# A decoder of four gated blocks: one-hot places by four comparisons, and the shared expert's fill in front of the slot list

## The chip, the cores and the metric

The kernel runs on one core of a Trainium2 chip. A core has TensorE (PE, matrix products into PSUM; PEld is its weight load), VectorE (DVE), ScalarE (ACT), GpSimd (POOL) and SyncE (SP), which work side by side and wait for one another by semaphores. DMA queues move data; GpSimd also issues the gathers. The metric is the device time of one launch in microseconds, lower is better. The kernel before takes 1079.16 us, the median of three runs (1078.13 to 1082.75).

## The reference

Sixteen blocks of 128 tokens with 256 features (`x`) pass through four pairs of a cross-attention-like layer and a feed-forward layer, each added to `x` with a learned gate:

```python
x = x + jnp.tanh(g_xattn[0]) * _L0_xattn_ref(ctx_2048, ctx_2048, _layernorm(x, axis=-1), ...)
x = x + jnp.tanh(g_ffn[0]) * _L0_ffn_ref(_layernorm(x, axis=-1), ...)
...
x = x + jnp.tanh(g_ffn[2]) * _L2_ffn_ref(_layernorm(x, axis=-1), ...)
```

Two of the feed-forward layers, number 0 and number 2, are mixtures of experts: for each of the 2048 tokens the two best of eight experts are taken, each expert is a gated product of width 176, and a shared expert that every token passes through is added. Number 2 in short:

```python
scores = jnp.sqrt(jax.nn.softplus(xt.astype(jnp.float32) @ gate_w.T))
_, idx = jax.lax.top_k(scores + gate_b, K)
weights = jnp.take_along_axis(scores, idx, axis=1) * ROUTE_SCALE
...
y = y + _expert(xt, w1[e], w2[e], w3[e], cw[:, e])   # for every expert e
z = _expert(xt, sw1, sw2, sw3)                       # the shared expert
return (y + z).reshape(Bx, Sx, D)
```

## The kernel before

The kernel goes through the eight layers as stages. The change lies in the two routed stages, `stage_moe0` (line 458, "stage one" in the prediction) and `stage_moe2` (line 739, "stage two"), and in the helper `spots` (line 387) that both call.

A routed stage does not multiply every token by every expert. It sorts token-expert pairs into 40 blocks of 128 slots, each block of one expert, gathers the tokens of a block from DRAM and multiplies them by that expert's weights. Its steps are:

- For four groups of four token blocks: `stats` and `normal` (VectorE; the power of -0.5 on GpSimd) write the normalised group `xn`, which SP also writes to DRAM (`xs`); `turn` transposes it on TensorE (tile `tx`) and copies it to `xT`; `logit` multiplies it by the gate weights into `lg`. In stage two `turn` also splits each value into a rounded part (ScalarE, line 736) and a rest (VectorE, line 737), and a group's scores are 16 products of 16 columns.
- `route`: from the scores the two best experts of each token (`first_two`), then `spots`. In stage two the route begins with three small functions on ScalarE (Exp at line 812, Ln, Exp), which are in VectorE's way.
- `spots`: the two best as a mask `mb`; TensorE counts by a triangular matrix (`pc`, line 395); from the counts come each pair's slot `ps`, its block `blk` and its place in the block `place`. Then the list of slots is made by a product: `inb` (line 421) says for each token and pair which of the 40 blocks it is in (128x1280, one or zero), `inp` (line 431) says for each token which of the 128 places it has, times the token's number. TensorE adds the 32 products into `w` (line 436): place by block, with the token's number in it. `who` (line 437) is that as an integer list, which steers the gathers (`load`, lines 593 and 848). `offs` (line 445) is the list of experts.
- The 20 double blocks: `load`, `block_turn` (tile `tb`), `block_up`, the hidden transposition (`tg`), `block_down` (`yb`).

The shared expert needs no list, so its work is cut into portions that are put where TensorE has to wait; the helper `fill` issues the next portion. In stage two there are ten portions for eight pairs of token blocks. Portion p multiplies pair p up (`up`, tile `ub`, eight products of 352 columns), transposes the hidden values of pair p-1 (`hidden`, tile `tg`) and multiplies pair p-2 down (`down`, tile `yb`). Unless a portion is called late, its hidden values go through ScalarE (`sil`, `gcopy`, two copies of `tg`, `ysh`) and GpSimd (`hid`, line 890; `hT`, line 905; the addition to `x`, line 941); a late one uses VectorE in GpSimd's place.

The order on TensorE, VectorE and ScalarE is the order of the calls in the source (`tc.manual_schedule`); each engine works off its instructions in that order. `route` and `spots` are generators: every `yield` is a place at which the caller may put a fill. In stage one a portion stands in each turn of the group loop, and the others around the route. In stage two before the change all ten portions stand behind the last scores: two behind the route's top, two behind the counts, two among the four rounds of `inp`, and the last four, late, behind the list.

PSUM tiles come from two pools: four buffers for `tx`, `lg`, `pc`, `w`, `tg` and `yb`, two for `ub`. `inp` has three buffers, shared with `xn`.

Of the kernel before, what the change touches and what calls it, by code (L numbers as in the profile page):

```python
# [10 lines left out]
F32 = mybir.dt.float32  # L11
# [3 lines left out]
ALU = mybir.AluOpType  # L15
# [3 lines left out]
P = 128  # L19
B = 16  # L20
# [35 lines left out]
def passage(ctx: ExitStack, tc: tile.TileContext, a: dict, out: bass.AP, inv, flag):  # L56
# [109 lines left out]
    def bc(ap, axis, n):  # L166

        u = ap.unsqueeze(axis)
        shape = list(u.shape)
        shape[axis] = n  # L170
        return u.to_broadcast(shape)
# [215 lines left out]
    def spots(mr, mo, psa, cn, one, pos, who, offs, inb):  # L387

        f, g = "p t e -> p (t e)", "p e t -> p (e t)"
        mb = mr.tile([P, B, E], BF16, name="mb")  # L390
        nc.vector.tensor_tensor(mb, one[:, 0], one[:, 1], ALU.add)
        yield
        pc = psa.tile([P, 2, B, E], F32, name="pc", tag="a")
        for i, w in enumerate((cn["upper"], cn["onesb"])):
            nc.tensor.matmul(pc[:, i].rearrange(f), lhsT=w, rhs=mb.rearrange(f), start=True, stop=True)
        cnt = mr.tile([P, E, B], F32, name="cnt")
        nc.vector.tensor_copy(cnt, pc[:, 1].rearrange("p t e -> p e t"))
        run = mr.tile([P, E, B], F32, name="run")
        nc.vector.tensor_tensor_scan(run.rearrange(g), cn["ct"].rearrange(g), cnt.rearrange(g), 0.0, ALU.mult, ALU.add)
        nb = mr.tile([P, E], F32, name="nb")  # L400
        nc.vector.tensor_scalar(nb, run[:, :, B - 1], 1.0 / P, 0.49609375, ALU.mult, ALU.add)
        nc.vector.tensor_scalar(nb, nb, MAGIC, None, ALU.add)
        nc.vector.tensor_scalar(nb, nb, MAGIC, None, ALU.subtract)
        be = mr.tile([P, E], F32, name="be")
        nc.vector.tensor_tensor_scan(be, ones[:, 0:E], nb, 0.0, ALU.mult, ALU.add)
        nc.vector.tensor_tensor(nb, be, nb, ALU.subtract)
        nc.vector.tensor_tensor(run, run, cnt, ALU.subtract)
        nc.vector.scalar_tensor_tensor(run, bc(nb, 2, B), float(P), run, ALU.mult, ALU.add)
        at = mr.tile([P, B, E], F32, name="at")
        nc.vector.tensor_tensor(at, pc[:, 0], run.rearrange("p e t -> p t e"), ALU.add)  # L410
        ps = mr.tile([P, 2, B], F32, name="ps")
        nc.vector.tensor_tensor(one, one, bc(at, 1, 2), ALU.mult)
        nc.vector.tensor_reduce(ps, one, AX.X, ALU.add)

        blk = mr.tile([P, 2, B], F32, name="blk")
        nc.vector.tensor_scalar(blk, ps, 1.0 / P, -0.49609375, ALU.mult, ALU.add)
        nc.vector.tensor_scalar(blk, blk, MAGIC, None, ALU.add)
        nc.vector.tensor_scalar(blk, blk, MAGIC, None, ALU.subtract)
        at = mr.tile([P, 2, B], F32, name="place")
        nc.vector.scalar_tensor_tensor(at, blk, -float(P), ps, ALU.mult, ALU.add)  # L420
        nc.vector.tensor_tensor(
            inb, bc(blk.rearrange("p i t -> p (i t)"), 2, NBLK), bc(cn["block"], 1, 2 * B), ALU.is_equal
        )
        yield

        w = psa.tile([P, NBLK], F32, name="w", tag="a")
        for q in range(0, 2 * B, 8):
            inp = mo.tile([P, 8, P], F32R, name="inp", tag="xn", bufs=3)
            for n in range(8):
                i, t = divmod(q + n, B)  # L430
                nc.vector.tensor_scalar(
                    inp[:, n], cn["slot"], at[:, i, t : t + 1], cn["token"][:, t : t + 1], ALU.is_equal, ALU.mult
                )
            yield
            for n in range(8):
                nc.tensor.matmul(w, lhsT=inp[:, n], rhs=inb[:, q + n], start=(q + n == 0), stop=(q + n == 2 * B - 1))
        nc.vector.tensor_scalar(who, w, B * P - 1.0, None, ALU.min)
        nc.vector.tensor_copy(pos, ps)

        le = mr.tile([1, NBLK, E], F32, name="le")  # L440
        jf = mr.tile([1, NBLK], F32, name="jf")
        nc.vector.tensor_tensor(le, bc(be[0:1], 1, NBLK), bc(cn["block"][0:1], 2, E), ALU.is_le)
        nc.vector.tensor_reduce(jf, le, AX.X, ALU.add)
        nc.vector.tensor_scalar(jf, jf, E - 1.0, float(WE), ALU.min, ALU.mult)
        nc.vector.tensor_copy(offs, jf)
# [293 lines left out]
    def stage_moe2(kv1, we, gw, gb, tgc, pos, wgt, cn, xs, ys):  # L739
# [4 lines left out]
        with tc.tile_pool(name="mr", bufs=1) as mr, tc.tile_pool(name="mo", bufs=2) as mo, tc.tile_pool(  # L744
# [34 lines left out]
            def turn(g):  # L779
                xn = xns.pop(g)  # L780
                for c in range(2):
                    t = psa.tile([P, GB * P], F32, name="tx", tag="a")
                    for k in range(GB):
                        nc.tensor.transpose(t[:, k * P : (k + 1) * P], xn[:, k, c * P : (c + 1) * P], ident)
                    split(xTs[g][:, c, 0], xTs[g][:, c, 1], t)
# [4 lines left out]
            def logit(g):  # L790
                for b in range(g * GB, (g + 1) * GB):
                    for n in range(4):
                        nc.tensor.matmul(
                            lg[:, b].rearrange("p a e -> p (a e)"),
                            lhsT=token(b, n // 2, n % 2),
                            rhs=gws[:, n // 2].rearrange("p a e -> p (a e)"),
                            start=(n == 0),
                            stop=(n == 3),
                        )
# [5 lines left out]
            def route():  # L805

                t3 = lambda n: mr.tile([P, B, E], F32, name=n)
                l, u, w, z, sc, sq, bi = [t3(n) for n in ("l", "u", "w", "z", "sc", "sq", "bi")]
                nc.vector.tensor_copy(l, lg[:, :, 1, :])
                nc.vector.tensor_tensor(l, l, lg[:, :, 0, :], ALU.add)  # L810
                nc.vector.scalar_tensor_tensor(u, l, -1.0, l, ALU.mult, ALU.max)
                nc.scalar.activation(u, u, AF.Exp, scale=-1.0)

                nc.vector.tensor_scalar(w, u, 1.0, None, ALU.add)
                nc.scalar.activation(sq, w, AF.Ln)
                nc.vector.tensor_scalar(w, w, -1.0, None, ALU.add)
                nc.vector.tensor_scalar(z, w, 0.0, None, ALU.is_equal)
                nc.vector.tensor_tensor(w, w, z, ALU.add)
                nc.vector.reciprocal(w, w)
                nc.vector.tensor_scalar(sc, l, 0.0, None, ALU.max)  # L820
                nc.vector.tensor_tensor(sq, sq, w, ALU.mult)
                nc.vector.tensor_tensor(sq, sq, z, ALU.add)
                nc.vector.tensor_tensor(u, u, sq, ALU.mult)
                nc.vector.tensor_tensor(sc, sc, u, ALU.add)

                nc.scalar.activation(sq, sc, AF.Ln)
                nc.scalar.activation(sq, sq, AF.Exp, scale=0.5)
                nc.vector.tensor_scalar(sq, sq, 1e-30, None, ALU.max)
                nc.vector.reciprocal(w, sq)
                nc.vector.tensor_tensor(w, w, sc, ALU.mult)  # L830
                nc.vector.tensor_tensor(sq, sq, w, ALU.add)
                nc.vector.tensor_scalar(sq, sq, 0.5, None, ALU.mult)
                nc.vector.tensor_tensor(bi, sq, bc(gb, 1, B), ALU.add)
                mx = mr.tile([P, 2, B], F32, name="mx")
                one = first_two(mr, cn, bi, mx, -BIG)
                yield
                gate = mr.tile([P, 2, B, E], F32, name="gate")
                nc.vector.tensor_tensor(gate, one, bc(sq, 1, 2), ALU.mult)
                nc.vector.tensor_reduce(wgt, gate, AX.X, ALU.add)
                nc.vector.tensor_scalar(wgt, wgt, tg[:, tgc : tgc + 1], None, ALU.mult)  # L840
                yield from spots(mr, mo, psa, cn, one, pos, who, offs, inb)
# [111 lines left out]
            for g in range(1, NG):  # L953
                if g + 1 < NG:
                    stats(g + 1)
                normal(g)
                logit(g - 1)
                turn(g)
            logit(NG - 1)
            r = route()  # L960
            next(r)
            fill()
            fill()
            next(r)
            next(r)
            fill()
            fill()
            for n in range(4):
                next(r)
                if n % 2 == 0:  # L970
                    fill()
            next(r, None)
            n = NBLK // 2
            for s in range(4):
                load(s)
# [1089 lines left out]
```

## Time and profile before

| What | us |
|---|---|
| median of three runs | 1079.16 |
| the profiled execution, its time | 1077.04 |
| its span, first to last instruction | 1075.3 |
| TensorE busy | 904.1 (84%) |
| VectorE busy | 607.5 (56%) |
| ScalarE busy | 456.8 (42%) |
| GpSimd busy | 342.3 (32%) |
| stage two: first `stats` | 584.2 |
| stage two: last scores end | 614.8 |
| stage two: `who` | 656.9 |
| stage two: first `tb` | 671.8 |
| stage one: last scores end | 166.0 |
| stage one: `who` | 195.5 |
| stage one: first `tb` | 207.5 |

A line of the timeline gives the start, the busy time, the engine, the source line, the operation, the tiles it writes and reads, the shape, and in brackets the idle time before it with what ended it. Busy times of pipelined matrix products overlap, so the distance from start to start is the better price of a piece. "PEclk" is the clock that TensorE was granted, as a share of the full one. The parts beside the stages in the table, the attention of the other layers, are not touched by the change.

### The profile page before, as it was taken

To read this page: it belongs to the slowest core of one execution; us is meant where nothing else is said; L and a number is where in the kernel's file an instruction comes from. 1 tells how busy PE (TensorE), PEld (TensorE's weight loads), DVE (VectorE), ACT (ScalarE), POOL (GpSimd) and SP (SyncE) were. 2 spreads that over 40 slices of the span, in tenths; PEclk is the share of its full clock that TensorE was granted. 3 is DMA by queue.
4 is the path that set the end of the run, shared out by engine and by line. 5 is a ranking of instruction groups with operands and counts; after the bars stand their busy time and mean duration, and the time that the engine had idled before them with its cause. 6 is when DMAs were issued, how large, how long until landed. Compare 5 with 4: busy or idle time off the path is not lost. (4 is left out here: it accounts for less than half of the span.)

```text
span 1075.3 us, 14892 instructions
## 1 busy us (share of the span) xinstructions
PE 904.1 (84%) x5212; PEld 602.5 (56%) x5212; DVE 607.5 (56%) x1537; ACT 456.8 (42%) x707; POOL 342.3 (32%) x389
## 2 busy tenths in 40 slices
PE   3899978899999888888864858998169999998797
PEld 1444456677778444455443747887145555555564
DVE  5988966322225656787788586454345555534442
ACT  1211024223322446666762242454257777882111
POOL 5766322543115324211111046550443342201000
PEclk9999979999999978999986557899579999997999
DMA  9100070233341109800000202352488887530000
GB/s 305 41 1 1 0 220 21 63 104 109 69 143 50 39 20 144 78 1 1 1 1 1 78 1 88 109 145 82 142 247 235 220 222 195 164 79 1 20 30 32
DMA packets 71401, 94.12 MB, mean 88 GB/s; under 512 B 9271, under 2 KB 63127, under 8 KB 69015
## 3 DMA queue, kind: packets, MB, share of 16 engines
q1 hardware_dynamic: 56952, 67.21, 21.1%
q0 software_dynamic: 14080, 23.78, 11.4%
q10 hardware_dynamic: 288, 2.10, 0.5%
q8 instruction: 45, 0.74, 0.3%
q14 instruction: 36, 0.29, 0.1%
HBM read 57.06 MB, written 33.55 MB: 84 GB/s over the span
## 5 line engine op out<-in xcount | busy, mean ns | idle before, releaser
L1667 ACT ACTIVATE pt<-s 128x1024 f32<-128x1024 f32 x128 | 126.4, 1024 | 32.5 <-PE s L1660 29.8
L709 POOL DMA_INDIRECT yc<-ys,pos x64 | 62.4, 975 | 125.0 <-DVE x L729 49.2
L297 PE MATMUL y<-kv,toep 128*128 128x512 f32 x192 | 86.6, 602 | 1.6 <-DVE toep L237 1.6
L1660 PE MATMUL s<-qa,ka 64*128 64x256 f32 x512 | 64.3, 332 | 8.3 <-ACT pt L1667 7.5
L1676 PE MATMUL av<-pt,v 128*32 128x256 f32 x1024 | 69.4, 389 | 0.1
L289 POOL TENSOR_TENSOR kv<-ctxT 128x1024 f32<-128x1024 f32 x32 | 60.2, 1900 | 28.3 <-PE y L297 28.3
L1660 PEld LDWEIGHTS s<-qa,ka 64*128 64x128 f32 x512 | 38.6, 188 | 46.9 <-issue 23.2
L1687 DVE COPY avs<-av 128x256 f32<-128x256 f32 x64 | 27.1, 423 | 65.5 <-PE av L1676 48.5
L297 PEld LDWEIGHTS y<-kv,toep 128*128 128x128 f32 x192 | 35.6, 192 | 43.7 <-issue 40.3
L616 PE MATMUL ub<-L0we,xbT 128*128 x160 | 50.8, 460 | 2.6 <-ACT xbT L607 2.6
L593 POOL DMA_INDIRECT xb<-xs,who x40 | 38.2, 954 | 43.3 <-PE tb L605 33.2
L913 PE MATMUL yb<-L2we,hT 88*128 (+1 forms) x224 | 41.7, 315 | 9.6 <-DVE hT L737 3.9
L848 POOL DMA_INDIRECT xb<-xs,who x40 | 38.1, 953 | 31.7 <-PE tb L860 20.9
L302 DVE TENSOR_TENSOR pr<-y,qT 128x1024 f32<-128x1024 f32 x32 | 39.0, 1222 | 12.1 <-PE y L297 9.4
L1567 POOL TENSOR_TENSOR hl<-f,hl 128x512 fp32r<-128x512 f32 x16 | 20.5, 1282 | 79.5 <-ACT hl L1566 79.5
L477 PE MATMUL up<-L0s,xT 128*128 128x352 f32 x128 | 43.0, 482 | 0.0
L913 PEld LDWEIGHTS yb<-L2we,hT 88*128 88x128 f32 x224 | 33.6, 205 | 16.5 <-DVE hT L737 9.0
L1086 PE MATMUL s<-qa,ka 18*128 18x512 f32 x128 | 37.4, 660 | 4.9 <-ACT follow L1380 4.9
L305 DVE TENSOR_REDUCE oT<-pr 128x128 f32<-128x1024 f32 x32 | 38.9, 1219 | 1.0
L1676 PEld LDWEIGHTS av<-pt,v 128*32 128x32 f32 x1024 | 26.9, 110 | 20.4 <-issue 0.7
L642 PE MATMUL yb<-L0we,hTb 88*128 x160 | 37.9, 379 | 0.0
L616 PEld LDWEIGHTS ub<-L0we,xbT 128*128 128x128 f32 x160 | 28.8, 190 | 15.5 <-ACT xbT L607 2.8
(384 smaller groups left out, 2043.1 us busy)
## 6 DMA issues: line engine op xcount, KB each, us to landing
scr<-hl SPq DMA_DIRECT2D x64, 256.0 KB
ys<-ysb SPq DMA_DIRECT2D x40, 256.0 KB
qa<-scr SPq DMA_DIRECT2D x32, 256.0 KB
ka<-scr SPq DMA_DIRECT2D x32, 256.0 KB
L2we<-in_L_w_dram POOLq DMA_DIRECT2D x6, 792.0 KB
L0we<-in_L_w_dram SPq DMA_DIRECT2D x6, 704.0 KB
xs<-xn SPq DMA_DIRECT2D x8, 512.0 KB
x<-in_x_dram SPq DMA_DIRECT2D x4, 512.0 KB
```

The costliest lines, as they stand in the source:

```text
L289: nc.gpsimd.tensor_tensor(t, bc(ch, 3, 8), bc(ch, 2, 8), ALU.mult)
L297: nc.tensor.matmul(y[:, ns], lhsT=T[:, h, d : d + P], rhs=kv[mc][:, ns], start=(mc == 0), stop=(mc == lc))
L302: nc.vector.tensor_tensor(pr, y.rearrange("p (b j i) -> p b j i", b=B, j=8), bc(qT[:, lc, :, hs], 2, 8), ALU.mult)
L305: nc.vector.tensor_reduce(oT[:, lc, :, hs], pr, AX.X, ALU.add)
L477: nc.tensor.matmul(t[:, n, 0 : 2 * I], lhsT=xT[:, c, b * P : (b + 1) * P], rhs=s13[:, c, n, :], start=(c == 0), stop=(c == 1),)
L593: nc.gpsimd.indirect_dma_start(out=xbs[s][:, i, :], out_offset=None, in_=xs, in_offset=bass.IndirectOffsetOnAxis(ap=who[:, 2 * s + i : 2 * ...
L616: nc.tensor.matmul(t[:, i, 0 : 2 * I], lhsT=xbT[:, i, c, :], rhs=we[:, bass.ds(regs[s][i] + c * 2 * I, 2 * I)], start=(c == 0), stop=(c == 1),
L709: nc.gpsimd.indirect_dma_start(out=got[b][:, i, :], out_offset=None, in_=ys, in_offset=bass.IndirectOffsetOnAxis(ap=pos[:, i, b : b + 1], ...
L913: nc.tensor.matmul(y[:, i, :], lhsT=hT[:, x, k, i, :], rhs=we[0:HI, bass.ds(at[i] + 4 * I + k * D, D)], start=(n == 0), stop=(n == 3),)
L1660: nc.tensor.matmul(s[:, h, jj, :], lhsT=ka[r, 2 * i + jj, sc * P : (sc + 1) * P], rhs=qa[r, 2 * i + jj, :], start=True, stop=True,)
L1667: nc.scalar.activation(pts[b, i][:, sc], s, AF.Exp)
L1676: nc.tensor.matmul(av[c : c + 32, :], lhsT=va[:, sc, 8 * h + 2 * i + jj, :], rhs=pt[:, sc, h, jj, :], start=(sc == 0), stop=(sc == 1),)
```

## The change

Two things are changed.

In `spots`, which both stages call, the token's number moves from `inp` to `inb`: two products of 128x640 in place multiply `inb` by it, and `inp` becomes a plain one-hot tile, made eight places at a time by one comparison of 128x1024 whose two operands are broadcast. Thirty-two instructions with two scalars each become four with two tensors each. TensorE's 32 products into `w` stay.

In `stage_moe2` the portions of the shared expert move. Two are now issued in each of the three turns of the group loop, one on either side of `turn`; one stands behind the last scores and in front of the route's top; the last three stand behind the route's top. From there the counts, `inb`, the four rounds of `inp` and the list follow with nothing between them. No portion is late any more, so all ten use ScalarE and GpSimd.

```diff
         nc.vector.tensor_tensor(
             inb, bc(blk.rearrange("p i t -> p (i t)"), 2, NBLK), bc(cn["block"], 1, 2 * B), ALU.is_equal
         )
+        for i in range(2):
+            u = inb[:, i * B : (i + 1) * B]
+            nc.vector.tensor_tensor(u, u.bitcast(F32), bc(cn["token"], 2, NBLK), ALU.mult)
         yield
 
         w = psa.tile([P, NBLK], F32, name="w", tag="a")
         for q in range(0, 2 * B, 8):
             inp = mo.tile([P, 8, P], F32R, name="inp", tag="xn", bufs=3)
-            for n in range(8):
-                i, t = divmod(q + n, B)
-                nc.vector.tensor_scalar(
-                    inp[:, n], cn["slot"], at[:, i, t : t + 1], cn["token"][:, t : t + 1], ALU.is_equal, ALU.mult
-                )
+            i, t = divmod(q, B)
+            nc.vector.tensor_tensor(inp, bc(at[:, i, t : t + 8], 2, P), bc(cn["slot"], 1, 8), ALU.is_equal)
             yield
...
                 normal(g)
                 logit(g - 1)
+                fill()
                 turn(g)
+                fill()
             logit(NG - 1)
             r = route()
+            fill()
             next(r)
             fill()
             fill()
-            next(r)
-            next(r)
             fill()
-            fill()
-            for n in range(4):
-                next(r)
-                if n % 2 == 0:
-                    fill()
-            next(r, None)
+            for _ in r:
+                pass
```

## The prediction

> **What bounds the kernel now.** I read the page first: the span, and the slices of TensorE's busy time and granted clock. "Slot list" below is the tile `who`; "stage one" is the first routed stage, "stage two" the second.
>
> ```profile
> span 1075.3 us, 14892 instructions
> PE   3899978899999888888864858998169999998797
> PEclk9999979999999978999986557899579999997999
> ```
>
> A slice is 26.9 us. TensorE is nearly full almost everywhere; the thin part is slices 22 to 26, which hold stage two, and there the clock is low as well. Then stretches of time (columns: length, busy us and instructions of PE, PEld, DVE, ACT, POOL, then PE clock, DMA share, GB/s), the last line from stage one:
>
> ```profile
> 595.70:602.00 6.30, 5.69 (x26) 5.00 (x25) 4.78 (x16) 1.17 (x2) 1.13 (x2) 0.50 0.26 86
> 620.00:626.00 6.00, 0.00 (x0) 0.00 (x0) 3.70 (x11) 3.99 (x6) 0.96 (x1) 0.50 0.00 0
> 150.00:155.00 5.00, 5.00 (x34) 4.10 (x33) 0.92 (x3) 1.97 (x5) 2.09 (x2) 1.00 0.99 248
> ```
>
> While stage two turns and scores the tokens, TensorE is busy 90% of the time yet has the half clock: so a slot that looks free there is not. During the top of the route it stands idle. The timeline of stage two gives the order of what ends last:
>
> ```profile
> 611.85 2.94 PE L793 MATMUL lg<-gws,xT 128*128 128x16 f32 x13 [0.26 <-DVE xT L737]
> 615.81 0.31 ACT L812 ACTIVATE u<-u 128x128 f32<-128x128 f32 x1 [3.44 <-DVE u L811]
> 631.74 0.29 PE L395 MATMUL pc<-mb,upper 128*128 128x128 bf16 x1 [2.13 <-DVE mb L391]
> 638.07 2.26 POOL L890 TENSOR_TENSOR hid<-gcopy,sil 128x352 f32<-128x352 f32 x1 [0.62 <-ACT gcopy L889]
> 639.47 17.07 DVE L431 TENSOR_SCALAR inp<-slot,place,token 128x128 fp32r<-128x128 f32 x32
> 656.91 0.20 DVE L437 TENSOR_SCALAR who<-w 128x40 uint32<-128x40 f32 x1 [0.38 <-PE w L436]
> 671.78 1.91 PE L860 MATMUL tb<-ident,xb 128*128 128x128 f32 x8
> ```
>
> From 614.8 to 656.9 VectorE carries the path. From 656.9 to 671.8 TensorE works off four fills and stands 3.30 us. From 689.8 the blocks run every 3.66 us at full clock. Stage one's timeline differs:
>
> ```profile
> 177.93 8.66 DVE L431 TENSOR_SCALAR inp<-slot,place,token 128x128 fp32r<-128x128 f32 x24
> 187.54 2.12 PE L436 MATMUL w<-inb,inp 128*128 128x40 f32 x16
> 188.81 2.75 DVE L431 TENSOR_SCALAR inp<-slot,place,token 128x128 fp32r<-128x128 f32 x8 [2.22 <-PE w L436]
> 195.48 0.20 DVE L437 TENSOR_SCALAR who<-w 128x40 uint32<-128x40 f32 x1 [3.92 <-PE w L436]
> ```
>
> There VectorE waits for TensorE, twice: 24 comparisons were ready at 186.6, TensorE came for them at 187.54.
>
> **Stage one: +0.5 us.** 32 comparisons (11.4 us in all) become two products of 128x640 and four comparisons of 128x1024. The row of `pr` (L302, same size) says 1.22 us for 1024, the row of `inb` (L421) 1.49 us for 1280, so by the line between them about 0.82 us for 640; started one behind another, 0.08 less each. The sum is 2x0.74 + 4x1.14 = 6.0 us. The 5.4 us saved are worth nothing, since the list waits for TensorE's fills. What may cost is GpSimd: its product beside the 1.49 us `inb` took 2.26 us where such a product otherwise takes 0.93, and here two of TensorE's waits (0.76 and 0.82 us) are for that product. One collision of a 1.14 us comparison with it is possible at 179.0. Bounds: -0.5 (no wait moves, VectorE's own interference gone) and +2 (two collisions); I take +0.5. The Trainium skill, "GPSIMD Engine Reference", section "Specifications", says the two engines share interfaces and that VectorE instructions with two SBUF inputs contend; all six new instructions are of that kind, so by that rule alone this term would be the +2.
>
> **Stage two, step by step.** Pieces of a fill, from one start to the next: `up` 2.49 us at half clock (634.46 to 636.95), 1.36 at full (645.91 to 647.27); `tg` 0.71 and 0.39; `yb` 1.86 and 1.05.
>
> *1. Six fills in the turning loop: +11.* They hold six `up`, five `tg`, four `yb`. At half clock that is 14.9+3.6+7.4 = 26 us on a TensorE already full: the upper bound. But fills are dense work, and stage one, with fills in the same loop, ran at 1.00. At full clock they cost 8.2+2.0+4.2 = 14.4, plus 2.1 for the first `up`, the first `tg` and half of the second `up` while still at half clock, plus 2 for two waits on the ScalarE-GpSimd chain (`yb` needs the second half of `hT`). Three sets of 16 scores fall from 4.37 us (597.77 to 602.14) to 1.70 (stage one, 150.38 to 152.08), and two turns from 1.99 to 0.88: -10.1. Net +8.4, the lower bound. After 16 small matmuls the clock can fall again: right after those of 647 to 650, a `tg` took 1.02 and an `up` 2.69, 1.55 us too much. I give that to nearly two of three groups: +11. VectorE's own loop (about 5.3 us a group) stays below TensorE's. The SP transfers of `xn` are issued from the same places, only later; the gathers need them 40 us on. On GpSimd's queue the fourth `rs` now stands behind three of the fills' products (about 1 us each); `normal` of the fourth group needs it some 5 us later, and `turn` after that. GpSimd's gathers are moved past nothing new: the fills' additions that stood ahead of them are done earlier.
>
> The rule and the row differ here: the Trainium skill, "TensorE: Matmul & The Clock Gate", section on the HAM clock gate, has the clock doubled after about 3.4 us of sustained activity; the trace shows 26 us of 90% busy time at 0.50, with matmuls of 16 columns in it. By the rule the loop would already be warm and this step would be near the full 14.4; by the row it is 8.4 to 26.
>
> *2. One fill in front of the route's first exponential: +4.* Exp (L812) now starts 1.0 us after the last score. ScalarE takes its work in order, so `sil` and `gcopy` of the seventh fill come first: 2.8 us of TensorE (1.05+0.39+1.36), 0.15 to its end, 0.8 for the two copies, and the table load of 1.28 us, hidden at 611.09 now, in the open: 5.0. Behind Exp waits the whole route on VectorE, and behind that `mb` and `pc`. Bounds +2 and +6 (half clock).
>
> *3. Counting behind the last fills: +2.* `pc` waits on TensorE behind the eighth to tenth fill. The eighth's copies stand in ScalarE's queue behind the route's last Exp, so from there: `ysh` 0.7, two copies 1.1, table 1.3, `sil` and `gcopy` 0.8, GpSimd 1.0; then `yb` and `tg` at half clock 2.6, two copies 1.1, GpSimd 1.3, `yb` 1.9: about 11 us, against 9 from that Exp to `mb` now (622.85 to 631.7). Bounds 0 and +4.
>
> *4. From the counts to `inb`: -0.7.* 5.9 us now, 4.6 in stage one, where GpSimd is quieter; one GpSimd addition remains beside it. Bounds -1.3 and 0.
>
> *5. From `inb` to the list: -7.2.* Now 18.85 us (638.06 to 656.91). After: `inb` 1.41, products 1.48, first comparison 1.14; then TensorE, idle for 9 us, multiplies 32 times. At half clock the nearest row is the scores' 0.226 us each (13 in 2.94): 7.2, which is slower than VectorE's comparisons; with 0.4 to the list, 11.7. At full clock (0.12 each) VectorE sets the end: 8.8. Bounds -10 and -7; I take half clock, as at 620 to 626 the same idleness has 0.50.
>
> *6. From the list to the first block: -9.2.* Now 14.9 us, because of the four fills. After, only the gathers: first at +0.48, second 1.45 later, data moving until 2.5 us after its issue (stage one: issued 195.96, moved until 198.5), and 1.3 for the 1 MB of `l3a` and `l3B` released at the same moment, which filled the DMA to 375 GB/s from 659.4: 5.7 in all. Bounds -10.4 and -8.
>
> *7. The first blocks: +1.5.* Turning of block 0 to that of block 5 takes 18.0 us now. After, gathers (2.5 us a block) are close ahead and TensorE starts at half clock: 16 to 21 us, so -2 to +3.
>
> **Sum.** 0.5 + 11 + 4 + 2 - 0.7 - 7.2 - 9.2 + 1.5 = +1.9 us on the profiled execution's 1077.04, so 1078.9. That execution lies 2.1 us below the median of the three timed runs, 1079.16; on that scale the prediction is 1081.
>
> **Rivals.**
> *The clock stays at half through the loop* (slower). Place: step 1; price: 26 instead of 11, and step 2 at 6 instead of 4: +19 in all, 1098. For it: 0.50 from 584 to 636 with the engine busy. Against it: stage one's 1.00 with fills between the same turns. From +16 in step 1 on it leaves the 0.5% band. Chance 0.27, partial forms included.
> *The list was the true limit* (faster). If the loop warms at once and stays so (8.4), `pc` does not wait (0) and the 32 products run at full clock (-10), the sum is -5.5, or 1073.7; with the first blocks at their lower bound too, -9.0, or 1070. I take 1072. For it: 42 us of VectorE path beside a TensorE that is often idle. Against it: that idleness is not filled, it is moved behind the fills. Chance 0.2.
> *The comparisons pay in stage one as well:* -5.4 more, 1075.5. Against it: the 3.92 us wait for `w`. Chance 0.04.
> That the change does not do what it says is excluded by the order of instructions: TensorE's fills do stand among turns and scores, and no fill is left behind `who`.
>
> **Numbers.** About 0.5%, 5.4 us, is what a measurement of this kernel can tell from no change. The summed case has 0.49; its steps reach their bounds in different directions, so I give it 1074 to 1086, of which 0.02 lies beyond the band on the slow side. With the other cases: faster by more 0.20, within 0.47+0.04 = 0.51, slower by more 0.27+0.02 = 0.29. The range leaves out the full cold loop and the best of the fast case: 1070 to 1093.
>
> **What would show it.** Right: stretches of the turning loop at 0.8 to 1.0 and the last score near 626; Exp 5 us behind it; four `inp` of about 1.2 us; `w` at 0.2 us each; first `tb` under 7 us after `who`; stage one's `who` still near 195.5. Wrong: a loop at 0.50 throughout, a `who` earlier than 657, a first block later than 675, or a stage one whose list moves by more than 2 us.

## The result, and the profile after

The changed kernel takes 1087.49 us (median of five runs, 1085.6 to 1089.4). The kernel before, measured beside it, takes 1080.0 (five runs, 1078.13 to 1082.75). The ratio is 1.0072, with a 95% interval of 1.0051 to 1.0092: slower by 0.7%, 7.5 us by the medians. The predicted range, 1070 to 1093, holds that time, but the case that was given 0.51, no change that can be told from none, did not come; "slower by more" had been given 0.29, for a reason that is not the one found.

The profiled execution of the changed kernel took 1089.4 us. Its page, the same lines as shown of the kernel before:

```profile
span 1087.6 us, 14864 instructions
PE   3899878899999888898864944698169999998796
PEclk9999988999999979999986875899579999998899
```

The slices are 27.2 us long now. Slice 23 has gone from busy 8 to 9 and its clock from 5 to 8: that is the turning loop with its fills. Slices 25 and 26, with the end of the list and the first blocks, have gone from 8 and 9 to 4 and 6, with clocks of 5 and 8 in place of 7 and 8. The next fence has stretches of the timeline (length, busy us and instructions of PE, PEld, DVE, ACT, POOL, then PE clock, DMA share, GB/s): four from the turning loop, then three from the first blocks.

```profile
605.00:610.00 5.00, 5.00 (x42) 5.00 (x41) 4.32 (x14) 2.85 (x7) 3.67 (x4) 1.00 0.00 0
610.00:615.00 5.00, 4.35 (x34) 4.12 (x32) 2.58 (x6) 3.90 (x9) 3.89 (x4) 1.00 0.30 105
615.00:620.00 5.00, 5.00 (x34) 4.77 (x33) 0.00 (x0) 2.62 (x6) 3.89 (x4) 0.80 0.32 108
620.00:625.00 5.00, 4.80 (x32) 4.56 (x32) 1.29 (x2) 3.46 (x7) 3.32 (x4) 0.86 0.00 0
680.00:685.00 5.00, 1.99 (x12) 1.51 (x11) 1.05 (x2) 0.58 (x1) 3.78 (x5) 1.00 0.35 105
685.00:690.00 5.00, 1.24 (x11) 1.00 (x9) 0.00 (x0) 0.34 (x1) 1.87 (x2) 0.63 0.26 79
690.00:695.00 5.00, 4.19 (x17) 4.15 (x18) 2.14 (x4) 2.13 (x5) 1.89 (x2) 0.50 0.34 105
```

The loop has the clock that the prediction hoped for, 0.80 to 1.00 where it was 0.50. But from 680 to 690 the core does nearly nothing except issue gathers: TensorE is busy 3.2 us of 10, VectorE 1.05, ScalarE 0.9. The timeline of the changed kernel (start, busy time, engine, line, tiles; in brackets the idle time before and what ended it), from the exponential to the stretch where it loses its time:

```profile
631.88 0.31 ACT L812 ACTIVATE u<-u 128x128 f32<-128x128 f32 x1
649.46 0.29 PE L395 MATMUL pc<-mb,upper 128*128 128x128 bf16 x1
658.39 4.62 DVE L433 TENSOR_TENSOR inp<-place,slot 128x1024 fp32r<-128x1024 f32 x4
659.75 6.99 PE L436 MATMUL w<-inb,inp 128*128 128x40 f32 x32 [9.90 <-DVE inp L433]
666.78 0.20 DVE L437 TENSOR_SCALAR who<-w 128x40 uint32<-128x40 f32 x1 [3.76 <-PE w L436]
671.71 0.45 PE L860 MATMUL tb<-ident,xb 128*128 128x128 f32 x1 [4.97 <-DMA xb<-xs,who]
683.27 0.58 ACT L736 CAST hT<-tg 88x512 fp32r<-88x512 f32 x1 [3.62 <-remote]
689.66 0.46 ACT L883 ACTIVATE sil<-ub 128x352 f32<-128x352 f32 x1 [5.81 <-remote]
690.81 1.08 PE L897 MATMUL tg<-ident,hid 128*88 128x128 f32 x4 [4.57 <-DVE hid L886]
699.70 0.60 PE L860 MATMUL tb<-ident,xb 128*128 128x128 f32 x4
```

Up to 671.71 everything is as the prediction has it. Then ScalarE waits twice, 3.62 and 5.81 us. "remote" means that the profile finds no instruction that ended shortly before the wait did: by its end in the profile, which is modelled for products, the one that `sil` reads was done at 681.3. The trace's record of semaphore updates tells more: both waits end with an update of the semaphore that TensorE alone raises, 1.9 and 3.4 us after the modelled end of the last product that raises it. So ScalarE waited for a signal of TensorE that came late. VectorE's `hid` waits for `sil`, TensorE's `tg` for `hid`. Block 5 is turned at 699.70, 28.0 us after the first, where it took 18.0 before:

```profile
689.78 0.60 PE L860 MATMUL tb<-ident,xb 128*128 128x128 f32 x4
```

Set beside each other, from the start of stage two (first `tx`: 589.34 before, 592.93 after):

| step of the prediction | predicted | measured (first two profiles) |
|---|---|---|
| 1 loop, to the last score | +11 | 25.45 to 34.02: +8.6 |
| 2 last score to Exp | +4 | 1.02 to 4.93: +3.9 |
| 3 Exp to `pc` | +2 | 15.93 to 17.58: +1.7 |
| 4 `pc` to `inb` | -0.7 | 6.32 to 5.93: -0.4 |
| 5 `inb` to `who` | -7.2 | 18.85 to 11.39: -7.5 |
| 6 `who` to the first `tb` | -9.2 | 14.87 to 4.93: -9.9 |
| 7 first `tb` to that of block 5 | +1.5 | 18.0 to 28.0: +10.0 |
| sum in stage two | +1.4 | 100.44 to 106.77: +6.3 |

Stage one's list (from `pc`, 171.59 and 171.93, to `who`, 195.48 and 196.19) takes 0.4 us longer, predicted +0.5. So one term failed, the last one. The profiles differ elsewhere as well: 3.2 us more ahead of stage two, and 3 in the last layer. Of the former, 1.6 are the first `ub` of stage one at a lower clock (4.18 us, 2.63 before), which two later executions of the changed kernel do not have. The rest lies in layers whose source the change does not touch, where executions differ by some us: from stage one's last `yb` to the start of stage two 275.3 to 276.7 us in three profiles of the kernel before (one of them with other buffers), 277.2 to 279.7 in the eleven of the changed kernel and all other versions below. The two groups part within 30 us, most of it between the `ts` (L1241 in the changed kernel) 64 to 65 us after that `yb` and the first `fu` (L1341), 89.3 to 89.9 us after it in the one and 91.3 to 92.8 in the other. Whether those 2 us come of the change, no run here tells; the comparisons alone have them too and are not slower as a whole.

### The profile page after: what moved, and what is told of

Its sections match the earlier page's. It is cut to its first block, busy times and chain, and to the rows that moved or that the text cites. A ratio compares the mean times of both kernels' runs of the same rounds, so it can differ in the third digit from the quotient of the medians.

```text
span 1087.6 us, 14864 instructions
## 1 busy us (share of the span) xinstructions
PE 899.0 (83%) x5212; PEld 596.6 (55%) x5212; DVE 588.7 (54%) x1476; ACT 460.5 (42%) x716; POOL 352.4 (32%) x398
```

## The experiments

Twelve runs were made, in four sittings, each with its own runs of the kernel before: 1064.12 us in sitting A, 1079.39 in B, 1080.81 in C, 1064.41 in D. Times are compared inside a sitting alone. B and D were on the same chip, so the two levels of the kernel before, 1064 and 1080, are not two chips; the first measurement is on the higher one. What tells them apart in a profile shows below. A difference in us that stands behind a ratio is worked out from the ratio, which need not be that of the two medians. In the tables and texts "to block 5" is the time from `who` of stage two to the turn of its block 5, from where on every block takes 3.6 to 3.7 us.

### One part alone: the comparisons

The changed `spots`, with stage two's fills where the kernel before has them. Against the changed kernel:

```diff
                 logit(g - 1)
-                fill()
                 turn(g)
-                fill()
             logit(NG - 1)
             r = route()
-            fill()
             next(r)
             fill()
             fill()
...
+            for n in range(4):
+                next(r)
+                if n % 2 == 0:
+                    fill()
```

> The comparisons alone (both stages), with stage two's fills where the kernel before has them. Theory A, the loss belongs to the moved fills: stage one's list +1.5 us as in the changed kernel; in stage two TensorE's fills and products now set the list, which comes 1 to 3 us earlier, and the turning loop, Exp and the first blocks (18 us from the turn of block 0 to that of block 5) stay as before: 0 us against the kernel before, -3 to +3. Rival B, the comparisons are the loss (VectorE's operations with two inputs from memory disturb GpSimd): +4 to +8 us, with GpSimd's products near 2 us in both stages.

Measured in sitting A: 1063.64 us, ratio 1.0 (0.9987 to 1.0013). The comparisons alone change nothing, as theory A had it, and the list of stage two still takes 19.3 us from `inb` (18.85 in the first profile). The cause is in two lines of this run's timeline, VectorE's comparisons and the list behind them, and in two of GpSimd's:

```profile
640.11 8.74 DVE L433 TENSOR_TENSOR inp<-place,slot 128x1024 fp32r<-128x1024 f32 x4
654.72 0.20 DVE L437 TENSOR_SCALAR who<-w 128x40 uint32<-128x40 f32 x1 [5.87 <-PE w L436]
```

```profile
643.32 2.24 POOL L941 TENSOR_TENSOR x<-x,ysh 128x512 f32<-128x512 f32 x1 [1.12 <-ACT ysh L940]
649.78 1.27 POOL L941 TENSOR_TENSOR x<-x,ysh 128x512 f32<-128x512 f32 x1
```

The four comparisons take 3.18, 1.21, 2.29 and 2.25 us beside GpSimd's work, and 1.22 each in the changed kernel, where GpSimd has nothing to do at that time; GpSimd's addition takes 2.24 us beside them and 1.27 behind them. The list is set by TensorE, which has two fills between the products, and VectorE waits 5.87 us for it. The Trainium skill, "SBUF — State Buffer", section "Who interferes with whom", says that a VectorE instruction with two inputs in SBUF contends with a GpSimd instruction that reads SBUF; these lines agree.

### The other part alone: the fills

The changed order of the fills with the 32 single comparisons:

```diff
-        for i in range(2):
-            u = inb[:, i * B : (i + 1) * B]
-            nc.vector.tensor_tensor(u, u.bitcast(F32), bc(cn["token"], 2, NBLK), ALU.mult)
...
-            i, t = divmod(q, B)
-            nc.vector.tensor_tensor(inp, bc(at[:, i, t : t + 8], 2, P), bc(cn["slot"], 1, 8), ALU.is_equal)
+            for n in range(8):
+                i, t = divmod(q + n, B)
+                nc.vector.tensor_scalar(
+                    inp[:, n], cn["slot"], at[:, i, t : t + 1], cn["token"][:, t : t + 1], ALU.is_equal, ALU.mult
+                )
```

> The moved fills alone, with the 32 single comparisons of the kernel before. Theory A: loop +8.5, Exp +4, counting +2, list -1 (17.1 us of comparisons stay, without fills between), list to first block -9, first blocks +10: +14 us against the kernel before, about 1094. Rival B (the comparisons carry the loss): 0 to +3 us.

Measured in sitting A: 1067.1 us, ratio 1.0026 (1.0017 to 1.0036), +2.8 us. Theory A named the right part and missed its size by 11 us; Rival B (0 to +3) has the size, but not the cause, since the comparisons alone cost nothing. Two terms of the expectation were wrong. The first blocks took 17.4 us and not 28, and no ScalarE wait marked "remote" is in this profile (nor in any of sitting A). And the list was faster than expected:

```profile
653.09 8.29 DVE L431 TENSOR_SCALAR inp<-slot,place,token 128x128 fp32r<-128x128 f32 x32
653.58 8.26 PE L436 MATMUL w<-inb,inp 128*128 128x40 f32 x32 [7.42 <-DVE inp L431]
661.87 0.20 DVE L437 TENSOR_SCALAR who<-w 128x40 uint32<-128x40 f32 x1 [0.49 <-PE w L436]
```

With no fill beside it, 32 single comparisons take 8.29 us, not 17.07, and TensorE follows them one by one: from `inb` (651.69) to the list 10.2 us. With four comparisons it is 11.4, because TensorE cannot begin before the two products and a whole group are through (4.4 us after `inb`, against 1.9) and then needs 7.0 us for 32 products. So what shortened the list in step 5 was that the fills left, and the four comparisons took 1.2 us of that back.

### Four fills behind the list

Six fills in the loop, none in the route, four behind the gathers as in the kernel before:

```diff
-            r = route()
-            fill()
-            next(r)
-            fill()
-            fill()
-            fill()
-            for _ in r:
+            for _ in route():
                 pass
```

> The changed kernel, but only the six fills of the turning loop stay ahead of the list; the other four stand behind the gathers, as in the kernel before. Theory A1, the first blocks' extra 10 us are a stall that four fills covered: the route starts 4 to 5 us earlier, the counting does not wait (-2), the first block is turned about where it is in the changed kernel, and from the turn of block 0 to that of block 5 18 us pass: 8 to 12 us less than the changed kernel, so 0 to -4 against the kernel before. Rival A2, the stall comes behind the fills as well (28 us for the first blocks): +5 to +8 against the kernel before.

Measured in sitting A: 1064.65 us, ratio 1.0005 (0.9996 to 1.0014), +0.5 us. Exp follows the last score by 1.0 us, `pc` follows Exp by 14.2, and the list stands 65.3 us after the start of stage two (73.9 in the changed kernel). Then the four fills take 12.6 us, block 5 is turned 27.9 us after the list, and the gain is gone. A2 is out; A1 has the time to within half a microsecond, but in this sitting there was no stall to cover.

### Fewer gathers in a row, stage two

Three buffers for gathered blocks in place of five:

```diff
-                xbs[s] = mo.tile([P, 2, D], F32, name="xb", bufs=5)
+                xbs[s] = mo.tile([P, 2, D], F32, name="xb", bufs=3)
...
-            for s in range(4):
+            for s in range(3):
                 load(s)
...
-                if 4 <= s + 4 < n:
+                if 3 <= s + 4 < n:
```

> The changed kernel with three buffers for the gathered blocks of stage two in place of five, so that GpSimd issues 6 gathers in a row in place of 16 and then waits for buffers. Theory A1g, ScalarE's waits of 3.6 and 5.8 us come from the long run of gathers: they go or move, and the first five blocks take 18 to 21 us in place of 28: 7 to 10 us less than the changed kernel. Rival, the run of gathers has no part in it (the clock, or something at a fixed distance behind the list): 27 to 30 us for the first blocks and no less time than the changed kernel.

Measured in sitting A: 1068.89 us, ratio 1.005 (1.0035 to 1.0065), +5.3 us. The first blocks took 17.9 us, with no wait of ScalarE above 2.4 us in them. That says nothing for theory A1g, since the three others in this sitting have five buffers (the comparisons alone with 20 gathers in a row in stage two) and no such wait either.

### Both kernels again

> The changed kernel once more, beside the others on one chip. Theory S: the runs with the moved fills so far show no wait of ScalarE above 2.4 us in the first blocks, which took 17.4 and 17.9 us; so the 28 us of the first profile belong to that chip's execution, not to the change, and the three buffers did not cure anything. Then this gives the moved fills' +3 us, plus 0.4 for the list of stage one and 1.2 for the list of stage two (11.4 us from inb to the list against 10.2 with single comparisons): +4 to +6 us, first blocks 17 to 19 us. Rival G: the run of 16 gathers brings the stall back: 27 to 29 us for the first blocks, and +7 us or more.

> The kernel before once more, for a profile on the same chip: no difference in time (0.999 to 1.001). Under theory S no wait of ScalarE over 3 us between gathers in either routed stage, and 15 us for the first blocks of stage two where its first profile showed 18.0.

Measured in sitting B: the changed kernel 1085.86 us, ratio 1.0062 (1.0044 to 1.0081), +6.7 us; the kernel before, against its own other runs, 1.0002 (0.998 to 1.0024). Theory S falls: the waits were back, and in both kernels. All waits that the tables of waits give as "remote", first of the changed kernel, then of the kernel before (engine, line, tile, what ended the wait: us in all, times, longest):

```profile
ACT hT L736 <- remote: 4.4, 1, 4.4
ACT sil L485 <- remote: 4.4, 1, 4.4
POOL xb L593 <- remote: 2.2, 1, 2.2
```

```profile
ACT sil L485 <- remote: 4.4, 1, 4.4
DVE x L937 <- remote: 2.5, 1, 2.5
POOL xb L593 <- remote: 2.2, 1, 2.2
```

The trace's semaphore updates say of all these waits what they said of the first: each ends with a late update of TensorE's semaphore. In stage one, in the first profile of the kernel before, three such updates, due at 207.7, 208.1 and 208.6 by the modelled ends, came at 210.12, 210.18 and 210.24; ScalarE's `sil` starts at 210.14, GpSimd's next gather at 210.44. Over the whole program, the last 5 us left out, each of the eight profiles on the level of 1080 has 30 to 34 updates of this semaphore more than 0.3 us behind the modelled end before them, up to 8.3 us, and every one of them during a gather of GpSimd or within 2.9 us of one; the six profiles on the level of 1064 have none. The eight also lack 23 to 28 of TensorE's 1002 to 1049 updates, and some of VectorE's and ScalarE's; the six lack none. Whether the recording itself is held up there, or causes the delay, no run here shows.

In stage one the wait is the same in both (L485). In stage two of the kernel before it stands among the late fills; there TensorE's timeline has

```profile
663.64 0.64 PE L897 MATMUL tg<-ident,hid 128*88 128x128 f32 x4 [0.20 <-issue]
668.85 2.59 PE L913 MATMUL yb<-L2we,hT 88*128 88x256 f32 x8 [4.57 <-issue]
671.24 1.91 PE L860 MATMUL tb<-ident,xb 128*128 128x128 f32 x8
```

A `yb` that takes 1.4 us at full clock waits 4.57 and then runs 2.59, so that a third of the 15.0 us between this list (656.24) and its first block is no work of the fills at all. In sitting A, with the same fills (the comparisons alone), the distance was 10.06.

### The exponential ahead of the seventh fill

```diff
             r = route()
-            fill()
             next(r)
+            fill()
             fill()
             fill()
             fill()
```

> The changed kernel with the route's first part (its exponentials and the choice of two experts) issued ahead of the seventh fill. Step 2 of the prediction says that the fill in front of Exp costs 4 us: Exp follows the last score by 1.0 us again. Then four fills stand between the last score and the counting; they hold two up, three tg and four yb, about 14 us at half clock, and their ScalarE work starts behind the last exponential, 7 us after the first. If VectorE's 15 us of route cover them, all 4 us come off the changed kernel; if the counting waits for them, 1 to 2 us. Not under 0.

Measured in sitting B: 1086.37 us, ratio 1.007 (1.0044 to 1.0097), and the changed kernel beside it 1.0062: nothing came off. Exp stands 1.0 us behind the last score (626.63), and yet `pc` is at 648.06, 55.4 us after the start of stage two, where the changed kernel has it at 55.5. TensorE shows why:

```profile
644.68 0.38 PE L913 MATMUL yb<-L2we,hT 88*128 88x256 f32 x1 [0.67 <-ACT hT L902]
646.88 1.38 PE L913 MATMUL yb<-L2we,hT 88*128 88x256 f32 x7 [1.81 <-POOL hT L905]
648.06 0.33 PE L395 MATMUL pc<-mb,upper 128*128 128x128 bf16 x1
```

The counting (`pc`) stands behind the last fill, and that waits for ScalarE and GpSimd. The four fills between the last score and the counting cost what they cost, whether Exp is in front of them or behind the first; only without them (49.2 us in the kernel with four fills behind the list) does the counting come earlier. The misses of steps 2 and 3 hide in a right sum.

### The last four fills at two places

```diff
             r = route()
-            fill()
             next(r)
             fill()
             fill()
-            fill()
             for _ in r:
                 pass
```

The ninth and tenth are then issued by the loop behind the gathers.

> The changed kernel with three places for the last four fills: the route's first part goes first, the seventh and eighth stand behind it, the ninth and tenth (which hold no up) behind the gathers. Exp at 1.0 us after the last score, counting 14.2 us after it, list 16.2 us after that, as with all four behind the list (list at 652 there); the two short fills take 4.5 us at half clock and 1.3 of waits, about the 5.1 us that TensorE stands for the first gather. So the first block is turned 5 to 6.5 us after the list, near 658, against 664.7 there and with the fills of before: 3 to 7 us less than the kernel before, if the first blocks do not lose more than 3 us to the half clock. Rival: every place costs the same work, and the time is the kernel before's within 2 us.

Measured in sitting B: 1083.31 us, ratio 1.0034 (1.0016 to 1.0053), +3.7 us. The list came 68.4 us after the start of stage two and the first block 5.8 us after the list, both as computed, but then two waits stood in the way:

```profile
677.20 0.59 ACT L736 CAST xbT<-tb 128x512 fp32r<-128x512 f32 x1 [4.50 <-remote]
683.57 0.58 ACT L736 CAST hT<-tg 88x512 fp32r<-88x512 f32 x1 [5.79 <-remote]
```

Block 2 was turned at 671.18, block 3 at 686.59. Of everything measured on this level, this one has the longest time from the list to block 5, 35.1 us: most of what the list gained, the waits took.

### Fewer gathers in a row, both stages

The edit of three buffers, made in `stage_moe0` as well, and the changed kernel a third time.

> The changed kernel a third time. If this chip shows the kernel before at about 1064 us (no waits of ScalarE between the gathers), the change costs +4 to +6 us: the moved fills' +3, 0.4 for stage one's list and 1.2 for stage two's. If the kernel before stands at about 1080, +6 to +8 us as before, with at least one wait of ScalarE over 3 us in the first blocks of stage two.

> The changed kernel with three buffers for gathered blocks in place of five in both routed stages, so that 6 gathers run in a row behind each list in place of 10 to 16. In stage one they are then all issued by about 204, while ScalarE's wait of 4.4 us ended at 210 in each run with the kernel before at 1080. Theory G (the long run of gathers makes the wait): on such a chip the wait at 206 to 210 goes or falls under 2.5 us, so do those of stage two, and the kernel takes 5 to 10 us less than the changed one. Rival (the wait has another cause): it stands at 206 to 210 as before, and the time is the changed kernel's within 2 us. On a chip without these waits both say: the changed kernel's time within 2 us.

Measured in sitting C: the changed kernel 1086.14 us, ratio 1.0057 (1.004 to 1.0074), +6.2 us. With three buffers 1076.65 us, ratio 0.9965 (0.9953 to 0.9976): 9.5 us under the changed kernel, and faster than the kernel before. Stage one first, where both kernels do the same work. ScalarE and GpSimd of the changed kernel:

```profile
209.57 0.46 ACT L485 ACTIVATE sil<-up 128x352 f32<-128x352 f32 x1 [4.43 <-remote]
209.87 0.95 POOL L593 DMA_INDIRECT xb<-xs,who  x1 [2.17 <-remote]
```

and with three buffers:

```profile
208.45 0.46 ACT L485 ACTIVATE sil<-up 128x352 f32<-128x352 f32 x1 [1.84 <-PE up L477]
209.13 0.95 POOL L593 DMA_INDIRECT xb<-xs,who  x1 [4.99 <-PE tb L605]
```

GpSimd issues six gathers until 204.1 and then waits 4.99 us for a buffer, and the same `sil` starts 1.84 us after ScalarE's last copy, as soon as its product is there. In stage two ScalarE's wait of 7.25 us in the changed kernel became one of 3.07, and the time from the list to block 5 fell from 32.9 to 25.0 us. The two waits of stage two, first of the changed kernel, then with three buffers, where the profile does name TensorE:

```profile
686.98 0.46 ACT L883 ACTIVATE sil<-ub 128x352 f32<-128x352 f32 x1 [7.25 <-remote]
680.05 0.46 ACT L883 ACTIVATE sil<-ub 128x352 f32<-128x352 f32 x1 [3.07 <-PE tb L860]
```

Theory G is shown for stage one, by one profile with six gathers in a row against seven with ten, and by the time: on this level it takes a long run of gathers to make the wait. In stage two, where the first transpositions free buffers early and 12 gathers still ran in a row, the wait is only shortened.

### Three buffers in the kernel before, and with the fills at two places

> The kernel before with three buffers for gathered blocks in both routed stages, nothing else. Theory G: where the kernel before stands at about 1080 it loses 2.3 us to ScalarE's wait in stage one and 3 to 4 in stage two, so this takes 4 to 7 us off it, and the changed kernel with three buffers (-4.2 against the kernel before) is then no better than this one: the change itself is worth -1 to +3 us without these waits. Rival: the three buffers help only the changed kernel, whose first blocks stand bare behind the list; then this is within 2 us of the kernel before. At 1064 for the kernel before: within 2 us of it by both.

> The changed kernel with the last four fills at two places (seventh and eighth behind the route's first part, ninth and tenth behind the gathers) and three buffers in both routed stages. The list comes 68.4 us after the start of stage two (73.9 in the changed kernel) and the first block 5.8 us after the list (4.9): 4.6 us less than the changed kernel with three buffers, so about 8 us less than the kernel before where that stands at 1080, and -3 to +1 where it stands at 1064. Rival: the fills cost the same wherever they stand, and it is within 2 us of the kernel before with three buffers.

Measured in sitting D, where the kernel before took 1064.41: 1063.98 us, ratio 0.9997 (0.9985 to 1.0009), and 1064.3 us, ratio 1.0002 (0.9992 to 1.0012). Without the waits three buffers change nothing, and neither do the fills' places, as the rival of the second had it: its list came 69.7 us after the start of stage two and its first block 5.8 us later, but it turned block 5 at 92.1 us, the kernel before with three buffers at 92.8. Of the 2.5 us that it was ahead at the first block, 1.9 went into the first blocks, at half clock (16.6 us from block 0 to block 5, against 14.7). What three buffers do for the kernel before on the other level was not measured.

### All of stage two in one table

| kernel | sitting | start to list | list to block 5 | both |
|---|---|---|---|---|
| before | first | 67.6 | 32.9 | 100.4 |
| before | B | 68.0 | 33.1 | 101.1 |
| changed | first | 73.9 | 32.9 | 106.8 |
| changed | B | 72.8 | 32.9 | 105.8 |
| changed | C | 73.9 | 32.9 | 106.8 |
| changed, Exp first | B | 72.6 | 31.6 | 104.2 |
| changed, fills at two places | B | 68.4 | 35.1 | 103.5 |
| changed, three buffers in both stages | C | 73.9 | 25.0 | 98.9 |
| comparisons alone | A | 68.0 | 24.8 | 92.9 |
| before, three buffers | D | 68.0 | 24.8 | 92.8 |
| four fills behind the list | A | 65.3 | 27.9 | 93.2 |
| fills alone | A | 71.6 | 22.7 | 94.3 |
| changed, three buffers in stage two | A | 73.8 | 23.0 | 96.9 |
| fills at two places, three buffers | D | 69.7 | 22.4 | 92.1 |

The first seven rows are on the level of 1080 with five buffers. There the list is followed by 33 us in the kernel before, which has four fills in that stretch, and by 33 us in the changed one, which has none. That is the result: on this level the fills behind the list were free. On the other level they cost 5 us there (27.9 us with four fills against 22.7 and 23.0 with none).

## Why the prediction was right or wrong

The signs that the prediction named all came: the loop at 0.80 to 1.00, Exp 4.9 us behind the last score, four `inp` of 1.2 us, `w` at 0.22 us each, the first block 4.9 us behind the list, stage one's list at 196.2. The latest place that any of them looks at is the first `tb`, and the time was lost behind it.

**Stage one, +0.5.** Measured +0.4 (23.9 to 24.3 us from `pc` to `who`, and 24.2 to 24.3 in all later runs with the new comparisons). The rival that the comparisons pay there is refuted.

**Step 1, +11.** Measured +8.6, at the lower bound, and 7.5 to 8.7 in the later runs with these fills in the loop (33.0 to 34.1 us, against 25.4 to 25.5). The rival of the cold loop is refuted: the first fill starts at 599.37, and from 604.4 on the clock is 1.00, with one fall to 0.50 from 618.0 to 621.4, behind 16 scores. That fall cost about 1.4 us (an `up` of 2.50 us in place of 1.37, a `tg` of 0.59 in place of 0.37, from start to start); two later executions of the changed kernel give 34.0 us with a fall and 33.0 without. So of the 2.6 us given to falls one half came, and the loop without them is 0.9 us cheaper than the lower bound.

**Steps 2 and 3, +4 and +2.** Measured +3.9 and +1.7, and the sum is near, in part by luck: the parts listed in step 3 add up to 11.8 us, not "about 11", and would have made it +3. The reason of step 2 is not right: with Exp back in its place the counting came no earlier. The price belongs to four fills, with their chain over ScalarE and GpSimd, ahead of the counting.

**Steps 4 and 5, -0.7 and -7.2.** Measured -0.4 and -7.5. Of step 5, the departure of the fills gives -8.7 (18.85 to 10.2 with the old comparisons), the new comparisons +1.2.

**Step 6, -9.2, and step 7, +1.5.** Here it failed, and on one reading. Step 6 took the 14.9 us between list and first block as the price of four fills; step 7 took the 18.0 us of the first blocks as the blocks' own, and added 1.5. The prediction itself quoted that TensorE "works off four fills and stands 3.30 us", and did not ask what the standing was. The profile before has it:

```profile
665.47 0.64 PE L897 MATMUL tg<-ident,hid 128*88 128x128 f32 x4
668.77 0.58 ACT L736 CAST hT<-tg 88x512 fp32r<-88x512 f32 x1 [3.91 <-remote]
669.40 2.58 PE L913 MATMUL yb<-L2we,hT 88*128 88x256 f32 x8 [3.30 <-issue]
```

While ten gathers ran one behind another, ScalarE waited 3.91 us for the `tg` that by its modelled end was done at 666.1; TensorE's signal came at 668.75. The `yb` behind it took 2.58 us at the low clock. The runs without these waits give the fills' real price between list and first block: 10.06 us against the 4.9 to 5.6 that the list's first gathers take with no fill, so step 6 was worth about 5 us. And the waits were never bound to the fills: with these gone, they fell into the first blocks, 28.0, 27.3 and 28.1 us in three executions against 17.4 and 17.9 without them. Steps 6 and 7 together were put at -7.7; they are 0.0 on this level, and about -2 on the other (24.8 to 23.0 or 22.7). Without the waits, then, the departure of the four fills is worth about 5 us, and the first blocks, which start at half clock behind a bare list, take 2.7 to 3.2 us longer (17.4 and 17.9 against 14.7).

With 0.0 in the place of -7.7, the prediction's own other terms as measured add up to +6.7 (0.4 + 8.6 + 3.9 + 1.7 - 0.4 - 7.5). By their ratios the three measurements are +7.8, +6.7 and +6.2. On the level of 1064 the changed kernel was not measured itself; with three buffers in stage two it is +5.3 (3.7 to 6.9), where the same sum gives 0.4 + 5.8 (start to list) - 1.8 (list to block 5), that is +4.4.

**The rivals.** None of the three is what came. Slower had been put on the clock; it was slower with the clock as hoped. That the time lies in the range is luck: the room on its slow side was made for a cold loop, and steps 1 to 5 with stage one, put at +9.6 and measured at +6.7, hid a part of the miss of 7.7. The case on the slow side that was missing is "the work behind the list was covering something": a wait that takes the place of the one removed.

What stays open: why TensorE's signals come late, and why at one time and not at another. In stage one the long wait takes the long run of gathers, and more than that, since in sitting A 16 to 24 gathers ran in a row without a late signal. Beside gathers in twos, in the last layer, the signals are late as well on the level of 1080, but only by 0.3 to 0.9 us. No transfer fills the DMA in that time (its share is 0.26 to 0.35 from 680 to 690). Since the ends of products are modelled, the trace can't tell whether the product was late or only its signal.

## What to carry to other kernels

When work is taken away in front of a stage, follow the sum to where the stage runs at its steady rate, not to its first instruction, and before work is priced by the stretch it stands in, subtract from that stretch every idle time that is not that work: here 5 of 15 us were a wait that came back elsewhere. Where a wait has no releaser in the profile, look at which engine's semaphore ended it. Replacing 32 small instructions by four large ones is no gain by itself where another engine consumes their results one by one; the consumer's first start counts. Where gathers run far ahead of their use, try fewer buffers: three in place of five cost the kernel before nothing in one sitting and gave the changed one 9.5 us in another.

## What the runs showed of the hardware

- On the level of 1080, TensorE's semaphore updates came 0.3 to 8.3 us after the modelled ends of its products beside GpSimd's gathers, 30 to 34 in each profile, often in threes 0.06 us apart; on the level of 1064 none did. Where GpSimd issued 10 to 16 gathers in a row, 1.25 us apart, the waits that ended with such an update were 2.4 to 7.2 us on ScalarE and 2.0 to 2.9 on GpSimd and VectorE. In stage one ScalarE's was 4.2 to 4.5 us in every profile on that level with ten in a row, of which the last 2.4 us or so lie behind the modelled end of its product; with six in a row it was 1.84, all of it before that end.
- The same kernel took 1064 and 1079 us on the same chip at different times. From the start of stage two to its last `yb` the kernel before takes 163.2 us on the one level (sitting B) and, with the same fills, 154.3 and 154.4 on the other; stage one's first block to block 2, 6.2 and 3.75; from stage two's last `yb` to the end 323.9 and 320.0, a stretch in which 22 to 25 of the late updates stand beside gathers. That is about all of the 15 us.
- Four VectorE comparisons of 128x1024 with two tensors took 1.22 us each alone and up to 3.18 beside GpSimd's products.
- TensorE's clock in the turning loop rose from 0.50 to between 0.80 and 1.00 when the fills, most of it products of 352 columns, were put among products of 16; without them it stayed at 0.50 while TensorE was 90% busy. The Trainium skill, "TensorE: Matmul & The Clock Gate", Part 1 on the HAM clock gate, has the full clock after about 3.4 us of sustained activity; the loop of the kernel before, all 25.5 us of it at 0.50, does not agree if busy time is the measure.
